# Edge weights of a message-passing layer: one product per tile on 64 rows of TensorE instead of a padded map

## The chip, the cores and the metric

One core of one Trainium2 chip. Its engines work side by side, each through its own list of instructions: PE (TensorE, matrix products; PEld is its loading of the stationary operand), DVE (VectorE), ACT (ScalarE), POOL (GpSimd) and SP (SyncE). Everything is float32. The metric is the device time of one execution in microseconds; the time given for a kernel is the median of several.

## The reference

There are 12,500 nodes with 160 features (64 scalars and 32 vectors of 3) and 400,000 edges, sorted by their target. Cut to what matters:

```python
h_s = s @ lin1_ws * a * inv(64)                  # per node
h_v = einsum('nci,cd->ndi', v, lin1_wv) * a * inv(32)
hid = silu(edge_scalars @ fc_w1 * inv(64))       # per edge, 64 numbers
w = hid @ fc_w2 * inv(64)                        # per edge, 224 edge weights
w1, w2, w3, w4, w5 = split(w, [64, 128, 160, 192])
es, ev = h_s[edge_src], h_v[edge_src]            # rows gathered by source
m_s1 = w1 * es * e0;  m_s2 = w4 * (ev . e1) * inv(3)
m_v1 = (w2 * es) x e1;  m_v2 = w3 * ev * e0;  m_v3 = w5 * cross(ev, e1) * inv(2)
agg = segment_sum(concat(m...), edge_dst) / 4    # 96 + 3*128 numbers per node
o = agg @ lin2 * a
y = layernorm(x + gate(self_connection + o))
```

`e0` and `e1` are an edge's four attributes. The change concerns the line `w = hid @ fc_w2`.

## The kernel before

**Start.** The node products `h_s`, `h_v` (L349, L359) are written as one table `h_tab` of 12,500 rows of 160 numbers to DRAM. POOL issues these writes, and after them the first gathers. DVE scales the map `fc_w2` into `w2` (L386), and subtracts the bases of blocks from the targets of all edges (`rel`, L420), which has to wait for `dt`, the targets.

**Tiles, chunks, quads.** A tile is 128 edges. Three tiles form a block, whose sums go into a window of 16 nodes. A chunk is 24 tiles, two halves of 12: half 0 holds the first 12 tiles, half 1 the next 12. The 64 inputs of half 0's edges lie on partitions 0 to 63 of `es`, those of half 1 on 64 to 127, so that one product with a block-diagonal `w1` and one `silu` (L463, L465) give `hid` for eight tiles, again with half 0 on the rows 0 to 63 and half 1 on 64 to 127. A step of the main loop takes a quad: two tiles of each half, four in all; `quads` lists them, and the place in that list is the tile's slot. There are 782 steps for 3,125 tiles, and the last step has one tile.

**One step n**, in the order in which the loop writes the instructions; on each engine they run in that order:

- POOL: four indirect gathers of 128 rows of `h_tab` into `hg` (L472), by the source of each edge. `hg` has four buffers, so the gathers may run four quads ahead of their use. In every 40th step (19 of them) the rows come by ordinary transfers instead, a row each, on the queues of SP and ACT (`hq`, L508), spread over the steps before.
- PE: the edge weights (L534) into `pw`, which has two buffers, so step n waits for DVE to be done with step n-2. `pw` is 4 x 256 float32 per partition, a slot for each tile: 224 weights, and 16 columns in which DVE writes the one-hot of targets (L597).
- DVE: the one-hot, the products `pr` of weights and gathered rows (L544 and three of L552), the select matrix `sel` (L606), and the addition of finished blocks into `acc` (L645).
- PE: the sums over targets of step n-2 (L613): each tile's `sel` (128x64) times its `pr` (128x416) into 64 of 128 partitions of `pa`, half 0's tiles into the first 64 and half 1's into the others, in turn.
- In every second step PE and ACT make `hid` for step n+2. When a block of each half is complete, ACT copies it (`sa`, L818), PE turns it (L622), ACT copies that (`tt`, L625, L627), and after 16 blocks PE applies `lin2` (L637). As nodes become complete, they are turned (L670), gated, normed and written out.

The stationary operand of the weights is `hid` of 128 rows, which has both halves' tiles one over the other. `w2` is therefore laid out twice with zeros: columns 0 to 223 have the map on rows 0 to 63, columns 224 to 447 have it on rows 64 to 127. One product of 128 rows and 448 columns then gives both tiles' weights, side by side in two neighbouring slots:

```python
nc.tensor.matmul(pw[:, t:t + m, :NWT], hid[:m * S, c * P:(c + 1) * P], w2[:m * S, :m], ...)
```

Of the kernel before, what the change touches and what calls it, by code (L numbers as in the profile page):

```python
# [10 lines left out]
F32 = mybir.dt.float32  # L11
# [10 lines left out]
P = 128  # L22
S = 64
# [12 lines left out]
CT = 2 * SIDE  # L36
# [11 lines left out]
NWT = 224  # L48
# [12 lines left out]
def gnn_kernel(  # L61
# [21 lines left out]
    nc = tc.nc  # L83
# [10 lines left out]
    consts = ctx.enter_context(tc.tile_pool(name="consts", bufs=1))  # L94
# [25 lines left out]
    def quads(halves):  # L120
        out = []
        for t in range(0, max(halves), 2):
            out.append([(half, u) for u in range(t, t + 2) for half in range(2) if u < halves[half]])
        return out


# [12 lines left out]
    for c, (_, halves) in enumerate(chunks):  # L139
        for i, slots in enumerate(quads(halves)):  # L140
            steps.append((c, i, [(tile_of(c, half, u), half, u) for half, u in slots]))
# [7 lines left out]
    def ahead(t):  # L149
        a0 = t // AHEAD * AHEAD  # L150
        if a0 not in aheads:
            n = min(AHEAD, TT - a0)
            idx = loads.tile([P, AHEAD], I32, name="idx")
            eat = loads.tile([P, AHEAD, 4], F32, name="eat")
            k = 0
            while k < n:
                g, u = divmod(a0 + k, GT)
                m = min(n - k, GT - u)
                nc.sync.dma_start(idx[:, k:k + m], src[g][:, u:u + m])
                nc.sync.dma_start(eat[:, k:k + m].rearrange("p t k -> p (t k)"),  # L160
                                  ea[g].rearrange("p t k -> p (t k)")[:, 4 * u:4 * (u + m)])
                k += m
            aheads[a0] = a0, idx, eat
        return aheads[a0]
# [5 lines left out]
    def by_slots(out, of, n, f):  # L170


        m = n // CT
        for u in range(SIDE if m else 0):
            o, i = out[:, 2 * u:2 * u + 1], of[:, u:u + 1]
            f(bass.AP(tensor=o.tensor, offset=o.offset,
                      ap=[o.ap[0], [CT * o.ap[1][0], m], [o.ap[1][0], 2], *o.ap[2:]]),
              bass.AP(tensor=i.tensor, offset=i.offset,
                      ap=[i.ap[0], [CT * i.ap[1][0], m], [SIDE * i.ap[1][0], 2], *i.ap[2:]]),
              u // BT, m)  # L180
        return m * CT
# [31 lines left out]
    w1 = consts.tile([2 * S, 2 * S], F32, name="w1")  # L213
    nc.vector.memset(w1, 0.0)

    w2 = consts.tile([2 * S, 2, NWT], F32, name="w2")
    nc.vector.memset(w2, 0.0)
    l2 = consts.tile([P, 11, V3], F32, name="l2")
    nc.vector.memset(l2, 0.0)
    share = ends_pool.tile([1, NB], I32, name="share")  # L220
# [10 lines left out]
    with tc.tile_pool(name="nodes", bufs=len(starts)) as nodes, tc.tile_pool(  # L231
        name="nodes_ps", bufs=6, space=PSUM
# [33 lines left out]
        for q in range(4):  # L266
            t0, s = divmod(q * QN, P)
            nc.gpsimd.dma_start(at_k[:P - s, q], attr[s:, t0:t0 + NQ])
            if s:
                m = min(NQ, NT - t0 - 1)  # L270
# [8 lines left out]
        at = consts.tile([P, NT], F32, name="at")  # L279
# [8 lines left out]
        halves = ends_pool.tile([P, 2], F32, name="halves")  # L288
# [32 lines left out]
        raw = ends_pool.tile([2 * S, NWT], F32, name="raw")  # L321
        for half in range(2):
            r = slice(half * S, (half + 1) * S)
# [14 lines left out]
        for c0, cn, xw, xz in loaded:  # L338
# [7 lines left out]
            n = min(cn, P)  # L346
# [32 lines left out]
    nc.vector.tensor_scalar_mul(half_at, at, 0.5)  # L379
    iota = consts.tile([P, W], F32, name="iota")  # L380
    nc.vector.tensor_copy(iota, iota_i)
    for half in range(2):
        r = slice(half * S, (half + 1) * S)
        at_c = 0
        for a, b in ((64, 128), (0, 64), (192, 224), (160, 192), (128, 160)):
            nc.vector.tensor_scalar_mul(w2[r, half, at_c:at_c + b - a], raw[r, a:b], 1.0 / math.sqrt(64))  # L386
            at_c += b - a

    scs = consts.tile([S, V3], F32, name="scs")
    nc.sync.dma_start(scs, sc_ws)  # L390
# [14 lines left out]
    for to, part, pieces, w, r0, c0, by in maps:  # L405
        for k, piece in enumerate(pieces):
# [3 lines left out]
            m = terms.setdefault((to, part, four), len(terms))  # L410
            at_r = at_p * V
            r = l2[at_r:at_r + V, m, c0:c0 + w.shape[1]]
# [11 lines left out]
    for t in range(by_slots(rel, dt, TT, relative), TT):  # L424
        nc.vector.tensor_tensor(rel[:, slot_of[t]:slot_of[t] + 1], dt[:, t:t + 1],  # L425
                                lo[:, t // BT:t // BT + 1], op=OP.subtract)
# [27 lines left out]
    def hidden(pool, psum, es, halves, t0, n):  # L454

        ph = psum.tile([2 * S, Q * P], F32, name="ph", tag="misc")
        hid = pool.tile([2 * S, Q * P], F32, name="hid")
        ends = [max(0, min(n, m - t0)) for m in halves]
        assert ends[0] >= ends[1]
        for k, c0, c1 in ((2 * S, 0, ends[1]), (S, ends[1], ends[0])):  # L460
            if c1 > c0:
                c = slice(c0 * P, c1 * P)
                nc.tensor.matmul(ph[:k, c], w1[:k, :k], es[:k, t0 * P + c0 * P:t0 * P + c1 * P],  # L463
                                 start=True, stop=True)
                nc.scalar.activation(hid[:k, c], ph[:k, c], AF.Silu, scale=1.0 / math.sqrt(64))  # L465
        return hid
# [59 lines left out]
    def weights(psum, hid, slots):  # L526

        pw = psum.tile([P, Q, 256], F32, name="pw")
        n = len(slots)
        for t in range(0, n, 2):  # L530
            half, c = slots[t]
            m = min(2, n - t)
            assert half == 0 and all(slots[t + k] == (k, c) for k in range(m))
            nc.tensor.matmul(pw[:, t:t + m, :NWT], hid[:m * S, c * P:(c + 1) * P], w2[:m * S, :m],  # L534
                             start=True, stop=True)
        return pw

# [33 lines left out]
    def by_slot(t):  # L571

        a0, _, eat = ahead(t)
        if a0 not in sorted_eat:
            n = min(AHEAD, TT - a0)
            eas = loads.tile([P, AHEAD, 4], F32, name="eas")
            m = n // CT
            for u in range(0, SIDE if m else 0, 2):
                o, i = eas[:, 2 * u:2 * u + 1], eat[:, u:u + 1]
                nc.scalar.copy(  # L580
                    bass.AP(tensor=o.tensor, offset=o.offset,
                            ap=[o.ap[0], [4 * CT, m], [8, 2], [4, 2], [1, 4]]),
                    bass.AP(tensor=i.tensor, offset=i.offset,
                            ap=[i.ap[0], [4 * CT, m], [4, 2], [4 * SIDE, 2], [1, 4]]))
            m *= CT
            for k in range(m, n):
                o = slot_of[a0 + k] - a0
                nc.scalar.copy(eas[:, o], eat[:, k])
            sorted_eat[a0] = eas
        return sorted_eat[a0]  # L590
# [10 lines left out]
    def select_quad(pool, tiles, oh):  # L601

        n = len(tiles)
        u = slot_of[tiles[0][0]] % AHEAD
        sel = pool.tile([P, Q, 4, W], F32, name="sel", bufs=3)
        nc.vector.tensor_mul(  # L606
            sel[:, :n], oh[:, :, None, :].to_broadcast([P, n, 4, W]),
            by_slot(tiles[0][0])[:, u:u + n, :, None].to_broadcast([P, n, 4, W]))
        return sel
# [108 lines left out]
    with tc.tile_pool(  # L718
        name="fin", bufs=1
    ) as fin, tc.tile_pool(  # L720
        name="mine", bufs=2
    ) as mine, tc.tile_pool(
        name="late", bufs=2
    ) as late, tc.tile_pool(name="edge", bufs=2) as edge, tc.tile_pool(
        name="deep", bufs=4
# [165 lines left out]
        with in_order:  # L891
# [6 lines left out]
            for n, (c, i, tiles) in enumerate(steps):  # L898
# [10 lines left out]
                fetch_rows(n)  # L909
                hg = hq_of.pop(n) if n in own else gather(deep, [index(t) for t, _, _ in tiles])  # L910
                pw = weights(pw_ps, hids[c, i // 2], [(half, u - i // 2 * 4) for _, half, u in tiles])

                rest = turning.pop(0)() if turning else None
# [46 lines left out]
            n = len(steps)  # L960
# [29 lines left out]
        with tc.For_i(0, n_redo, 1):  # L990
# [9 lines left out]
            with tc.For_i(0, n_again, 1) as g, tc.For_i(0, GT, 1) as k:  # L1000
                t = g * GT + k
# [19 lines left out]
                hid = hidden(edge, misc_ps, es, (1, 0), 0, 1)  # L1021
                hg = gather(deep, [idx])
                pr = products(edge, weights(pw_ps, hid, [(0, 0)]), hg, 1)
                r = edge.tile([P, 1], F32, name="r", bufs=1)
                had = edge.tile([P, 2], F32, name="had", bufs=1)
# [73 lines left out]
```

## Time and profile before

| | us |
|---|---|
| median of 3 runs | 3920.53 (3918.47 to 3926.07) |
| the profiled execution | 3915.52 |
| span of its instructions | 3913.8 |
| PE busy | 3634.4 (93%) |
| POOL busy | 2915.6 (74%) |
| DVE busy | 2441.2 (62%) |
| ACT busy | 895.3 (23%) |
| granted clock of TensorE, mean | 0.972 |

A row of a timeline has the start and the length of a piece of work in us, the engine, the line, the operation, what it writes and reads, its shape and how often it follows on itself; in square brackets stands how long the engine was idle before it and what ended that. A row of a group has, behind the bar, the busy time in us and the mean in ns of one, then the idle time ahead of it. A float32 product leaves two records on PE.

### The profile page before, as it was taken

The page shows a single profiled execution, that of the slowest core. Times are in us where ns is not written, and L with a number is a line of the kernel's source. Part 1 is how long each engine was busy: PE and PEld are TensorE (multiplying, and loading weights), DVE is VectorE, ACT ScalarE, POOL GpSimd, SP SyncE. Part 2 cuts the span into 40 slices and gives each one's busy share as a digit, 9 for nine tenths or more (in the row PEclk, how much of TensorE's full clock was granted, in tenths as well). Part 3 has the DMA queues.
Part 4 walks back from the last instruction along what each step waited for, and adds up shares of the span by engine and source line. Part 5 has one row for each costly group of instructions (what it writes and reads, how often), then busy time and mean ns, then how long its engine had stood idle before and what let it go on. Part 6 is the DMA issues. An engine that isn't in the chain of part 4 may idle for free. (4 is left out here: it accounts for less than half of the span.)

```text
span 3913.8 us, 66881 instructions
## 1 busy us (share of the span) xinstructions
PE 3634.4 (93%) x14293; PEld 1589.8 (41%) x14293; DVE 2441.2 (62%) x6532; ACT 895.3 (23%) x2481; POOL 2915.6 (74%) x3096
## 2 busy tenths in 40 slices
PE   6899999999989999899899999989999999989998
PEld 4344344344334444344344343434444344334443
DVE  6656566666655666656566666656666665656655
ACT  2222222222222222222222222222222222222222
POOL 6777777777777777777777777777777777777774
PEclk8999999999999999999999999999999999999999
DMA  7344444444344443443444444444343443444432
GB/s 241 97 104 104 101 105 101 101 105 105 101 105 103 105 108 99 104 109 98 103 106 103 101 109 101 102 103 107 101 111 98 101 112 98 102 103 100 104 99 65
DMA packets 258055, 413.16 MB, mean 106 GB/s; under 512 B 92568, under 2 KB 186273, under 8 KB 257509
## 3 DMA queue, kind: packets, MB, share of 16 engines
q0 software_dynamic: 149312, 260.41, 25.7%
q1 hardware_dynamic: 98004, 145.13, 15.1%
q10 hardware_dynamic: 10322, 3.26, 0.4%
q14 instruction: 302, 2.47, 0.2%
q8 instruction: 115, 1.88, 0.2%
HBM read 392.53 MB, written 16.00 MB: 104 GB/s over the span
## 5 line engine op out<-in xcount | busy, mean ns | idle before, releaser
L472 POOL DMA_INDIRECT hg<-h_tab,idx x3049 | 2885.1, 946 | 942.6 <-issue 834.8
L534 PE MATMUL pw<-w,hid 128*128 128x448 f32 x3126 | 1346.2, 554 | 29.3 <-ACT hid L465 10.8
L613 PE MATMUL pa<-pr,sel 128*64 128x416 f32 x6250 | 1287.4, 533 | 0.2 <-ACT sa L818 0.2
L552 DVE TENSOR_TENSOR pr<-pw,hg 128x384 f32<-128x384 f32 x2289 | 1125.7, 547 | 0.0
L597 DVE TENSOR_TENSOR pw<-rel,iota 128x64 f32<-128x64 int16 x782 | 181.4, 232 | 956.4 <-PE pw L534 953.4
L534 PEld LDWEIGHTS pw<-w,hid 128*128 128x128 f32 x3126 | 553.5, 193 | 487.4 <-issue 420.3
L544 DVE TENSOR_TENSOR pr<-pw,hg 128x512 f32<-128x512 f32 x763 | 527.1, 691 | 346.3 <-DMA hg<-h_tab,idx 250.9
L613 PEld LDWEIGHTS pa<-pr,sel 128*64 128x64 f32 x6250 | 384.4, 138 | 799.0 <-issue 772.9
L818 ACT COPY sa<-pa 128x416 f32<-128x416 f32 x521 | 262.8, 505 | 1081.3 <-DMA hq<-h_tab 612.7
L463 PE MATMUL misc<-es,w 128*128 128x512 f32 (+1 forms) x784 | 446.2, 651 | 20.3 <-DVE rel L425 17.7
L465 ACT ACTIVATE hid<-misc 128x512 f32<-128x512 f32 x392 | 233.5, 596 | 784.0 <-DMA hq<-h_tab 379.3
L622 PEld LDWEIGHTS misc<-ident,sa 128*128 128x128 f32 x2084 | 242.8, 143 | 383.9 <-issue 254.9
L622 PE MATMUL misc<-ident,sa 128*128 128x128 f32 x2084 | 334.1, 284 | 69.2 <-ACT hid L465 56.6
L637 PE MATMUL misc<-tt,l 128*96 128x256 f32 (+5 forms) x1496 | 360.7, 390 | 32.9 <-DVE y L683 26.9
L606 DVE TENSOR_TENSOR sel<-pw,eas 128x256 f32<-128x256 f32 x782 | 324.3, 415 | 9.5 <-ACT eas L580 9.3
L637 PEld LDWEIGHTS misc<-tt,l 128*96 128x96 f32 (+1 forms) x1496 | 233.8, 168 | 179.1 <-issue 98.3
L625 ACT COPY tt<-misc 128x192 f32<-128x192 f32 x521 | 164.6, 316 | 559.8 <-DMA hq<-h_tab 371.4
L463 PEld LDWEIGHTS misc<-es,w 128*128 128x128 f32 x784 | 118.4, 190 | 282.9 <-issue 229.8
L645 DVE TENSOR_TENSOR acc<-acc,os 96x32 f32 x1042 | 195.6, 188 | 25.3 <-ACT os L640 6.8
L627 ACT COPY tt<-misc 128x64 f32<-128x64 f32 x521 | 117.1, 225 | 0.0
L670 PE MATMUL misc<-ident,acc 96*128 96x96 f32 x196 | 35.5, 266 | 77.2 <-DVE pw L597 46.4
L640 ACT COPY os<-misc 96x512 f32<-96x512 f32 (+2 forms) x68 | 38.3, 563 | 208.6 <-PE misc L637 202.3
(89 smaller groups left out, 672.8 us busy)
## 6 DMA issues: line engine op xcount, KB each, us to landing
es<-in_es_t_dram SPq DMA_DIRECT2D x258, 384.0 KB
hq<-h_tab SPq DMA_DIRECT2D x4864, 0.6 KB
hq<-h_tab ACTq DMA_DIRECT2D x4864, 0.6 KB
hg<-h_tab,idx POOLq DMA_INDIRECT x3049
h_tab<-ht POOLq DMA_DIRECT2D x24, 320.0 KB
xt<-in_x_dram SPq DMA_DIRECT2D x23, 320.0 KB
out_dram<-y SPq DMA_DIRECT2D x23, 320.0 KB
xv<-in_xv_t_dram SPq DMA_DIRECT2D x25, 187.5 KB
```

The lines of the kernel that those rows point to most:

```text
L463: nc.tensor.matmul(ph[:k, c], w1[:k, :k], es[:k, t0 * P + c0 * P:t0 * P + c1 * P], start=True, stop=True)
L465: nc.scalar.activation(hid[:k, c], ph[:k, c], AF.Silu, scale=1.0 / math.sqrt(64))
L472: nc.gpsimd.indirect_dma_start(out=hg[:, t, :], out_offset=None, in_=h_tab, in_offset=bass.IndirectOffsetOnAxis(ap=i, axis=0))
L534: nc.tensor.matmul(pw[:, t:t + m, :NWT], hid[:m * S, c * P:(c + 1) * P], w2[:m * S, :m], start=True, stop=True)
L544: nc.vector.tensor_mul(two, pw[:, :n, :2 * S].rearrange("p t (k c) -> p t k c", k=2), hg[:, :n, None, :S].to_broadcast([P, n, 2, S]))
L552: nc.vector.tensor_mul(pr[:, :n, first:first + V3].rearrange("p t (i c) -> p t i c", i=3), pw[:, :n, None, 2 * S + k * V:2 * S + (k + 1) * ...
L606: nc.vector.tensor_mul(sel[:, :n], oh[:, :, None, :].to_broadcast([P, n, 4, W]), by_slot(tiles[0][0])[:, u:u + n, :, None].to_broadcast([P ...
L613: nc.tensor.matmul(pa[half * ROWS:(half + 1) * ROWS, :NPR], sel[:, t].rearrange("p k w -> p (k w)"), pr, start=start, stop=stop)
L622: nc.tensor.transpose(pt[:, four * P:four * P + k], sa[:k, c:c + P], ident[:k, :k])
L637: nc.tensor.matmul(po[:, k, :nb], l2[r, terms[to, part, four]], a[:, :nb], start=(n == 0), stop=(n == len(of) - 1))
L645: nc.vector.tensor_add(window, window, os[:, :, b])
L818: nc.scalar.copy(sa, pas.pop(j)[:, :NPR])
```

## The change

The map `w2` is kept without zeros: once on rows 0 to 63 and once on rows 64 to 127, 224 columns. Each tile has a product of its own, of the 64 rows of its half and 224 columns. `quads` now lists both tiles of half 0 and then both of half 1, so the slots 0 and 1 of `pw` belong to half 0 and the slots 2 and 3 to half 1; the products are issued in the order of tiles u, half 0 before half 1, which is slots 0, 2, 1, 3. The lists that go by slots (`rel`, and the attributes `eas`) are written in the new order, and the gathers of a quad follow it. The sums over targets keep their order.

```diff
     def quads(halves):
         out = []
         for t in range(0, max(halves), 2):
-            out.append([(half, u) for u in range(t, t + 2) for half in range(2) if u < halves[half]])
+            out.append([(half, u) for half in range(2) for u in range(t, t + 2) if u < halves[half]])
         return out
...
         for u in range(SIDE if m else 0):
-            o, i = out[:, 2 * u:2 * u + 1], of[:, u:u + 1]
+            at = u // 2 * 4 + u % 2
+            o, i = out[:, at:at + 1], of[:, u:u + 1]
             f(bass.AP(tensor=o.tensor, offset=o.offset,
-                      ap=[o.ap[0], [CT * o.ap[1][0], m], [o.ap[1][0], 2], *o.ap[2:]]),
+                      ap=[o.ap[0], [CT * o.ap[1][0], m], [2 * o.ap[1][0], 2], *o.ap[2:]]),
...
-    w2 = consts.tile([2 * S, 2, NWT], F32, name="w2")
-    nc.vector.memset(w2, 0.0)
+    w2 = consts.tile([2 * S, NWT], F32, name="w2")
...
-    for half in range(2):
-        r = slice(half * S, (half + 1) * S)
-        at_c = 0
-        for a, b in ((64, 128), (0, 64), (192, 224), (160, 192), (128, 160)):
-            nc.vector.tensor_scalar_mul(w2[r, half, at_c:at_c + b - a], raw[r, a:b], 1.0 / math.sqrt(64))
-            at_c += b - a
+    at_c = 0
+    for a, b in ((64, 128), (0, 64), (192, 224), (160, 192), (128, 160)):
+        nc.vector.tensor_scalar_mul(w2[:, at_c:at_c + b - a], raw[:, a:b], 1.0 / math.sqrt(64))
+        at_c += b - a
...
         pw = psum.tile([P, Q, 256], F32, name="pw")
-        n = len(slots)
-        for t in range(0, n, 2):
-            half, c = slots[t]
-            m = min(2, n - t)
-            assert half == 0 and all(slots[t + k] == (k, c) for k in range(m))
-            nc.tensor.matmul(pw[:, t:t + m, :NWT], hid[:m * S, c * P:(c + 1) * P], w2[:m * S, :m],
+        for t, (half, c) in sorted(enumerate(slots), key=lambda k: (k[1][1], k[1][0])):
+            r = slice(half * S, (half + 1) * S)
+            nc.tensor.matmul(pw[:, t, :NWT], hid[r, c * P:(c + 1) * P], w2[r],
                              start=True, stop=True)
         return pw
...
-                            ap=[o.ap[0], [4 * CT, m], [8, 2], [4, 2], [1, 4]]),
+                            ap=[o.ap[0], [4 * CT, m], [4, 2], [8, 2], [1, 4]]),
```

## The prediction

> **What bounds the kernel now.** I read the page first, for shares and groups, then everything about the gather line, then timelines of the start, the steady part and the end.
>
> ```profile
> span 3913.8 us, 66881 instructions
> PE 3634.4 (93%) x14293; PEld 1589.8 (41%) x14293; DVE 2441.2 (62%) x6532; ACT 895.3 (23%) x2481; POOL 2915.6 (74%) x3096
> ...
> L534 PE MATMUL pw<-w,hid 128*128 128x448 f32 x3126 | 1346.2, 554 | 29.3 <-ACT hid L465 10.8
> ...
> L606 DVE TENSOR_TENSOR sel<-pw,eas 128x256 f32<-128x256 f32 x782 | 324.3, 415 | 9.5 <-ACT eas L580 9.3
> ```
>
> And of the view of waits:
>
> ```profile
> DVE pw L597 <- PE pw L534: 953.4, 601, 9.7
> ```
>
> By the shares PE is the bound; L534, the line that is changed, is its largest group, and DVE's longest wait is for it (953.4 us in 601 times). The view of the gather line L472 says otherwise:
>
> ```profile
> L472 POOL DMA_INDIRECT hg<-h_tab,idx x3049: 940/946/1100, 51.2 to 3874.5; - x191
> ...
>   issue: 834.8, 2720
> ```
>
> A gather takes 0.946 us and POOL then sits 0.31 us (834.8 / 2720) in "issue", waiting for nothing that the trace shows. The stretches view over 480 gathers, cut at gather starts (columns: us, then busy us and count of PE, PEld, DVE, ACT, POOL, then clock, DMA share, GB/s):
>
> ```profile
> core 0: us, PE busy (x) PEld busy (x) DVE busy (x) ACT busy (x) POOL busy (x), PEclk, DMA share, GB/s
> 2410.90:3011.44 600.54, 564.25 (x2206) 243.13 (x2206) 376.39 (x1002) 134.97 (x386) 454.13 (x480) 0.98 0.41 102
> ```
>
> 600.54 / 480 = 1.251 us per gather. 3048 intervals of that are 3813.1 us; from first to last gather the rows give 3874.5 - 51.2 = 3823.3. So POOL stalls only 10.2 us in the whole run. The time is 51.2 (before the gathers) + 3813.1 + 10.2 + 39.3 (3913.8 - 3874.5). A faster PE can touch only the last two terms; nothing in the change shortens a gather, and their number stays 3049. Of the 10.2 us, two stalls as POOL's timeline shows them:
>
> ```profile
> 70.04 0.94 POOL L472 DMA_INDIRECT hg<-h_tab,idx  x1 [0.30 <-issue]
> 74.48 0.97 POOL L472 DMA_INDIRECT hg<-h_tab,idx  x1 [3.50 <-DVE l L307]
> ...
> 3524.89 0.95 POOL L472 DMA_INDIRECT hg<-h_tab,idx  x1 [0.30 <-issue]
> 3528.54 0.94 POOL L472 DMA_INDIRECT hg<-h_tab,idx  x1 [2.70 <-issue]
> ```
>
> The first is the start: four buffers `hg` are full, and gather 17 waits for the first products; 4.44 - 1.25 = 3.2 us. That leaves 7.0 us in the middle, of which the second pair is 2.4.
>
> **How far the consumers are behind.** DVE's products (L544) and POOL's gathers near the end:
>
> ```profile
> 3763.28 0.94 POOL L472 DMA_INDIRECT hg<-h_tab,idx  x1 [0.30 <-issue]
> ...
> 3868.29 0.95 POOL L472 DMA_INDIRECT hg<-h_tab,idx  x1 [0.30 <-issue]
> ...
> 3873.29 0.94 POOL L472 DMA_INDIRECT hg<-h_tab,idx  x1 [0.30 <-issue]
> 3874.53 0.94 POOL L472 DMA_INDIRECT hg<-h_tab,idx  x1 [0.30 <-issue]
> ```
>
> ```profile
> 3765.93 0.69 DVE L544 TENSOR_TENSOR pr<-pw,hg 128x512 f32<-128x512 f32 x1 [1.83 <-DMA hg<-h_tab,idx]
> ...
> 3884.09 0.68 DVE L544 TENSOR_TENSOR pr<-pw,hg 128x512 f32<-128x512 f32 x1
> 3884.69 1.48 DVE L552 TENSOR_TENSOR pr<-pw,hg 128x384 f32<-128x384 f32 x3
> ...
> 3886.55 0.28 DVE L544 TENSOR_TENSOR pr<-pw,hg 128x128 f32<-128x128 f32 x1
> 3886.75 0.58 DVE L552 TENSOR_TENSOR pr<-pw,hg 128x96 f32<-128x96 f32 x3
> ```
>
> At 3765.93 DVE waits for the gather issued at 3763.28: 2.65 us from issue to use is the least. The last whole quad (gather 3873.29) is used at 3884.09, 10.8 us behind, 8.15 more than needed; the last tile 12.0 behind. This backlog, made by PE, is what the change can take from the end.
>
> **The product itself.** PE's timeline, one steady step and the last steps:
>
> ```profile
> 1002.84 1.67 PE L534 MATMUL pw<-w,hid 128*128 128x448 f32 x4
> ...
> 1004.44 1.62 PE L613 MATMUL pa<-pr,sel 128*64 128x416 f32 x8
> ...
> 1005.98 0.66 PE L622 MATMUL misc<-ident,sa 128*128 128x128 f32 x4
> ```
>
> ```profile
> 3878.13 1.67 PE L534 MATMUL pw<-w,hid 128*128 128x448 f32 x4
> 3879.73 1.62 PE L613 MATMUL pa<-pr,sel 128*64 128x416 f32 x8
> 3881.28 0.66 PE L622 MATMUL misc<-ident,sa 128*128 128x128 f32 x4
> ...
> 3885.51 0.64 PE L534 MATMUL pw<-w,hid 64*128 64x224 f32 x2
> 3886.10 2.44 PE L637 MATMUL misc<-tt,l 128*96 128x96 f32 x22
> 3888.38 0.60 PE L622 MATMUL misc<-ident,sa 128*128 128x128 f32 x4
> 3888.91 2.31 PE L613 MATMUL pa<-pr,sel 128*64 128x416 f32 x10
> ```
>
> One f32 product leaves two records. A quad's four records of 448 columns take 1.60 us (1002.84 to 1004.44): about 0.375 each and 0.1 to drain before L613. The kernel has one 64-row product already, its last: two records of 224 columns, 0.59 us (3885.51 to 3886.10), weight load and drain with it. A record of 224 columns streams half as long as one of 448, 0.187. After the change a quad has eight such records, four on rows 0-63 and four on rows 64-127. If the halves overlap, it is 0.59 + 2 x 0.187 = 0.96 us, and up to 0.1 more where the step before was a full-array one (a drain like that ahead of L613): 0.55 to 0.64 less per quad, some 470 us of PE over 781 quads. If they don't, 0.59 + 6 x 0.187 = 1.71 with loads hidden, and 4 x 0.59 = 2.36 with none hidden.
>
> I take the overlap, by the nearest row: L613's eight records (two column halves of the array, each with its own load) take 1.54 us (1004.44 to 1005.98); at 416/448 x 0.375 = 0.35 each, one after another, they would need 2.8. That is columns, not rows: no row here has two row halves at once. The Trainium skill (TensorEngine Tiling (Array Packing), Key Properties and Gotcha 1) says that tiles operate in parallel, and that different row tiles cannot use one PSUM bank together; the new listing puts slots 0, 1 (half 0) and 2, 3 (half 1) into different 2 KB of `pw`. By that page the sum is the 0.96; no run here shows it.
>
> **What it is worth, end by end.** Beginning:
>
> ```profile
> 67.69 3.35 PE L534 MATMUL pw<-w,hid 128*128 128x448 f32 x4 [0.69 <-ACT hid L465]
> ```
>
> ```profile
> 58.30 6.23 DVE L420 TENSOR_TENSOR rel<-dt,lo 128x260 int16<-128x260 int32 x12 [11.79 <-DMA dt<-in_dst_dram]
> ...
> 71.08 0.23 DVE L597 TENSOR_TENSOR pw<-rel,iota 128x64 f32<-128x64 int16 x1 [6.22 <-PE pw L534]
> ```
>
> At the slow clock of the start the first product takes 67.69 to 71.08. Half the columns on the path are 1.5 us less, and POOL's stall of 3.2 shrinks by that: -1.5 (ends 0 and -3.2). Middle: consumers that run 2.65 us behind instead of 6 to 12 seldom fill four buffers. But the stall at 3524.89 comes from ACT, which the change doesn't touch:
>
> ```profile
> 3508.60 11.50 ACTq L508 DMA_DIRECT2D hq<-h_tab  x9
> 3520.20 0.60 ACT L465 ACTIVATE hid<-misc 128x512 f32<-128x512 f32 x1 [11.18 <-DMA hq<-h_tab]
> ```
>
> Nine row transfers hold ACT's queue for 11.5 us, and `hid` is late. Such a lump still fits into the buffers more often than now: -5 of 7.0 (ends 0 and -7). End: the last whole quad can be used at 3873.29 + 2.65 = 3875.94, 8.15 earlier. PE has then to be ready too. The quad before (last gather 3868.29) is used at 3870.94, and its products and select end 2.5 later (3884.09 to the end of L552 is 2.08, and 0.415 of L606): 3873.4. From there PE has L613 1.55, L622 0.66, the 64-row product 0.59, L637 2.28 and L622 0.53, 5.6 us, so L613 of the last quads could start at 3879.0 instead of 3888.91: 9.9 earlier. The last tile's products end at 3887.33 - 8.15 = 3879.2, in time for their place in that L613. I take -8.5, less by one half-clock stretch (below; 1.7 us), with the ends 0 and -9.9.
>
> Edits at nothing: ten scalings of `w2` become five and a memset goes, all ahead of DVE's wait of 11.79 for `dt`. The gathers, row transfers and eas copies change order, not number or size. The twelve `rel` subtractions (6.23 us, on the path to the first product) now write every second slot instead of pairs: taken as 0; ends -1 and +6. Eight weight loads instead of four are in the 0.59. The path after a failed margin doesn't run.
>
> Sum: 1.5 + 5 + 8.5 = 15.0 off a span of 3913.8: 3898.8; the profiled execution of 3915.52 becomes 3900.5. The median of the runs, 3920.53, lies 5.0 above that execution. What a run has beyond it can only be more stalls of POOL or a later end, the terms that shrink, so I let half of it go too: 3920.5 - 15 - 2.5 = **3903 us**, 0.45% less. 0.2% (7.8 us) is about what a measurement of this kernel can tell from no change.
>
> **Rivals.** *Halves one after another* (slower). PE idles 36.3 us in the 600.54 above, which is 120 gathered quads and 3 fetched otherwise: 0.295 us a step. A product over 1.60 + 0.295 = 1.90 us makes PE the bound. With every load exposed 2.36 + 0.09: 0.55 over, x 782 = 430 us: 4350. With loads hidden, 1.71 to 1.8, it stays under the point with 0.1 to 0.2 a step to spare; the backlog is cleared more slowly and the 7.0 us of stalls can double or treble: 3925 to 3940. For it: nothing shows row halves together; against: the column halves do it.
>
> *The clock gives it back.* PE will idle more. Successive stretches of 3.41 us:
>
> ```profile
> 1120.73:1124.14 3.41, 2.64 (x12) 1.18 (x13) 0.92 (x2) 1.45 (x5) 2.49 (x3) 1.00 0.38 110
> 1124.14:1127.55 3.41, 1.50 (x7) 0.59 (x7) 2.80 (x10) 0.43 (x2) 2.50 (x4) 1.00 0.22 62
> 1127.56:1130.97 3.41, 3.41 (x9) 0.99 (x6) 3.20 (x8) 0.22 (x1) 2.57 (x3) 0.50 0.28 74
> ```
>
> A stretch with PE busy 1.50 of 3.41 is followed by one at half clock. A light step after the change (0.96 + 1.55 of POOL's 5.0) leaves 2.5 us idle, so there will be more of these; each costs PE 1.7 us of work. Two at the end take 3.4 back (3906); if the whole gain of the end and the 2.5 of the median go, 3914. The skill (TensorE: Matmul & The Clock Gate, Part 1) names an idle window of about 3.4 us as the condition; the trace shows that a part-idle one does it, and that is what counts here.
>
> *The ends don't move.* Products in the end are held by something beside PE (accumulating, DMA landing), and start and middle bring under 7.8: 3913 to 3920.
>
> **How the numbers follow.** Forecast 0.64; clock 0.14 (0.10 of it beyond 7.8 us); ends 0.10; halves in turn 0.12. Faster 0.74, same 0.14, slower 0.12. Range: low with all ends at once, 3920.5 - 3.2 - 7 - 9.9 - 5 = 3895; high 3916, into the third rival; left out is the first and part of the third.
>
> **What would show it.** Right: L534 as 64x224, eight records in about 1 us with starts in pairs a few ns apart; gathers still 1.251 apart; first stall under 2; L544's last quad about 2.7 us after its gather; PE near 80%; more half-clock stretches. Wrong: starts of the records 0.19 or more apart, PE over 93%, DVE's wait for `pw` not below 953 us, or a last gap that stays at 10.

## The result, and the profile after

| | before | after |
|---|---|---|
| median of runs, first comparison, us | 3921.74 (3916.14 to 3926.07, 8 runs) | 3911.73 (3909.36 to 3912.68, 8 runs) |
| median of runs, a second chip, us | 3916.83 (3910.18 to 3920.85, 16 runs) | 3903.96 (3901.75 to 3904.91, 7 runs) |
| span of the profiled execution, us | 3913.8 | 3910.0 |
| PE, DVE, POOL busy, us | 3634.4, 2441.2, 2915.6 | 3322.2, 2413.3, 2925.1 |
| granted clock of TensorE, mean | 0.972 | 0.928 |

The ratio after / before is 0.9974 [0.9963, 0.9985] in the first comparison and 0.9967 [0.9956, 0.9979] on the second chip: faster, by 10.0 and 12.9 us, on both. The prediction was 3903. Two sets of the experiments ran on chips on which every kernel, the kernel before too, takes 5300 to 5700 us; their times are compared only with the kernel before on the same chip.

From the page of after, its head and two groups (busy us, mean ns, idle ahead and what ended it):

```profile
span 3910.0 us, 73124 instructions
PE 3322.2 (85%) x17417; PEld 1636.5 (42%) x17417; DVE 2413.3 (62%) x6526; ACT 894.0 (23%) x2481; POOL 2925.1 (75%) x3096
...
L470 POOL DMA_INDIRECT hg<-h_tab,idx x3049 | 2894.3, 949 | 935.3 <-issue 811.1
...
L529 PE MATMUL pw<-w,hid 64*128 64x224 f32 x6250 | 859.8, 391 | 194.8 <-DVE sel L601 98.7
```

From the view of waits of after (us in total, times, longest):

```profile
DVE pr L539 <- DMA hg<-h_tab,idx: 543.5, 261, 6.2
DVE pw L592 <- PE pw L529: 484.4, 264, 9.0
```

The lines have moved up by two to five: L529 is the weights product (L534 before), L470 the gather, L539 and L547 the products, L592 the one-hot, L418 the `rel` subtractions, L608 the sums, L506 the row transfers.

The weights product costs PE 859.8 us instead of 1346.2, 486 less. Other work takes 174 more of PE's busy time, some two thirds of it because it ran longer at half clock (below), and the busy time as a whole fell by 312 us. DVE waits for PE half as long (484.4 against 953.4), and its longest wait is now for the rows of the gathers. The run became only 4 us shorter in this profile. The gather line says why: 0.949 us per gather where the profile before had 0.946, with the same pause after it. The bound is the one of before, and in this profile it had itself become slower.

The stretch of 600.54 us in which the profile before had PE busy 564.25:

```profile
2410.90:3011.44 600.54, 519.30 (x2690) 253.47 (x2690) 368.06 (x992) 134.20 (x383) 454.36 (x480) 0.93 0.41 103
```

Again 480 gathers run in it, with PE idle 81 us in place of 36.

The product itself, in PE's timeline of after:

```profile
3863.16 1.03 PE L529 MATMUL pw<-w,hid 64*128 64x224 f32 x8
3864.11 1.62 PE L608 MATMUL pa<-pr,sel 128*64 128x416 f32 x8
```

Eight records follow on each other in 0.95 us, where four of 448 columns took 1.60. Single records show how: they start at 3863.155 and .162, .448 and .455, .637 and .644, .827 and .833. Two run at once, one per half. After the first pair, which has 0.29 to itself, a pair follows the one before by 0.19, the time of 224 columns. The Trainium skill (TensorEngine Tiling (Array Packing), Key Properties) says that different tiles can run LdWeights and Matmul in parallel; this trace agrees for row halves in float32, with 0.958 us per quad.

The start, on PE and DVE of after, and POOL's first stall:

```profile
70.13 1.86 PE L529 MATMUL pw<-w,hid 64*128 64x224 f32 x8 [0.69 <-ACT hid L463]
```

```profile
59.80 7.31 DVE L418 TENSOR_TENSOR rel<-dt,lo 128x260 int16<-128x260 int32 x12 [11.56 <-DMA dt<-in_dst_dram]
66.91 0.38 DVE L423 TENSOR_TENSOR rel<-dt,lo 128x1 int16<-128x1 int32 x5
```

```profile
72.04 0.94 POOL L470 DMA_INDIRECT hg<-h_tab,idx  x1 [0.30 <-issue]
75.48 0.95 POOL L470 DMA_INDIRECT hg<-h_tab,idx  x1 [2.49 <-DVE l L307]
```

The first product takes 1.86 in place of 3.35, and the stall is 2.19 beyond a normal interval, 3.2 before. The subtractions take 7.31 in place of 6.23.

The end, DVE and POOL and then PE, of after:

```profile
3877.60 0.95 POOL L470 DMA_INDIRECT hg<-h_tab,idx  x1 [0.30 <-issue]
3878.86 0.94 POOL L470 DMA_INDIRECT hg<-h_tab,idx  x1 [0.30 <-issue]
```

```profile
3880.38 0.68 DVE L539 TENSOR_TENSOR pr<-pw,hg 128x512 f32<-128x512 f32 x1
...
3882.72 0.28 DVE L539 TENSOR_TENSOR pr<-pw,hg 128x128 f32<-128x128 f32 x1
```

```profile
3884.76 2.31 PE L608 MATMUL pa<-pr,sel 128*64 128x416 f32 x10
```

The last whole quad is used 2.8 us after its gather (10.8 before), the last tile 3.9 (12.0 before), and the last sums start 5.9 us after the last gather (14.4 before). What lies behind the last gather fell from 39.2 to 31.1 us.

Where the 3.8 us of span went, from POOL's rows of both profiles: the first gather came 1.9 later (51.18 to 53.12; over all profiles here it lies between 51.2 and 53.3, without regard to the kernel); the stall of the start gave 1.0; the stalls of the middle (intervals over 1.3 us, less 1.251 each) fell from 7.7 to 2.5, which gave 5.2; the end gave 8.1. That is 14.3 less 1.9. Against it, the mean of the ordinary intervals is 1.25366 us in place of 1.25081: over 3048 of them, 8.7 us.

### The profile page after: what moved, and what is told of

Read it like the earlier page. It is cut to its first block, busy times and chain, and to the rows that moved or that the text cites. A ratio compares the mean times of both kernels' runs of the same rounds, so it can differ in the third digit from the quotient of the medians.

```text
span 3910.0 us, 73124 instructions
## 1 busy us (share of the span) xinstructions
PE 3322.2 (85%) x17417; PEld 1636.5 (42%) x17417; DVE 2413.3 (62%) x6526; ACT 894.0 (23%) x2481; POOL 2925.1 (75%) x3096
## 5 line engine op out<-in xcount | busy, mean ns | idle before, releaser
L470 POOL DMA_INDIRECT hg<-h_tab,idx x3049 | 2894.3, 949 | 935.3 <-issue 811.1
L608 PE MATMUL pa<-pr,sel 128*64 128x416 f32 x6250 | 1359.9, 559 | 1.8 <-ACT sa L813 1.8
L547 DVE TENSOR_TENSOR pr<-pw,hg 128x384 f32<-128x384 f32 x2289 | 1125.7, 547 | 0.0
L539 DVE TENSOR_TENSOR pr<-pw,hg 128x512 f32<-128x512 f32 x763 | 527.2, 691 | 816.6 <-DMA hg<-h_tab,idx 543.5
L529 PE MATMUL pw<-w,hid 64*128 64x224 f32 x6250 | 859.8, 391 | 194.8 <-DVE sel L601 98.7
L529 PEld LDWEIGHTS pw<-w,hid 64*128 64x128 f32 x6250 | 567.2, 195 | 493.8 <-issue 233.2
L608 PEld LDWEIGHTS pa<-pr,sel 128*64 128x64 f32 x6250 | 400.0, 143 | 579.5 <-issue 561.7
L461 PE MATMUL misc<-es,w 128*128 128x512 f32 (+1 forms) x784 | 465.9, 678 | 44.5 <-ACT tt L622 26.1
L592 DVE TENSOR_TENSOR pw<-rel,iota 128x64 f32<-128x64 int16 x782 | 180.2, 230 | 492.4 <-PE pw L529 484.4
L617 PE MATMUL misc<-ident,sa 128*128 128x128 f32 x2084 | 343.3, 289 | 131.2 <-ACT hid L463 102.2
L667 ACT ACTIVATE g<-misc,half_at 128x96 f32<-128x96 f32 x98 | 33.4, 341 | 224.0 <-PE misc L665 122.4
```

The lines of the kernel that those rows point to most:

```text
L470: nc.gpsimd.indirect_dma_start(out=hg[:, t, :], out_offset=None, in_=h_tab, in_offset=bass.IndirectOffsetOnAxis(ap=i, axis=0))
L529: nc.tensor.matmul(pw[:, t, :NWT], hid[r, c * P:(c + 1) * P], w2[r], start=True, stop=True)
L539: nc.vector.tensor_mul(two, pw[:, :n, :2 * S].rearrange("p t (k c) -> p t k c", k=2), hg[:, :n, None, :S].to_broadcast([P, n, 2, S]))
L547: nc.vector.tensor_mul(pr[:, :n, first:first + V3].rearrange("p t (i c) -> p t i c", i=3), pw[:, :n, None, 2 * S + k * V:2 * S + (k + 1) * ...
L608: nc.tensor.matmul(pa[half * ROWS:(half + 1) * ROWS, :NPR], sel[:, t].rearrange("p k w -> p (k w)"), pr, start=start, stop=stop)
L617: nc.tensor.transpose(pt[:, four * P:four * P + k], sa[:k, c:c + P], ident[:k, :k])
```

## The experiments

**The same two kernels on a second chip.** The question was whether the 3 ns per gather are the change's.

> The kernel before, unchanged. On the chip of the first four experiments every kernel took 5380 us or more, with register moves of 0.03 us on SP's queue that took up to 1.4 us there, so the question of the gather interval stayed open: both kernels had 1.2506 there. Theory A (0.003 us more per gather belongs to an execution or a chip, not to the kernel): on a chip where the kernel before takes about 3920, the two means of gather intervals agree to 0.001 us. Theory B: 1.2508 here and 1.2537 in the changed kernel.

> The changed kernel, unchanged. Theory A: the mean gather interval is that of the kernel before here to 0.001 us; the last gap is 31 against 39 us, the stalls of POOL 5 against 11 us, and the time 12 to 15 us less. Theory B: 0.003 us longer per gather, 8.7 us of the gain gone, 6 to 10 us less.

Before: 3914.49, ratio to the other runs of the kernel before 0.9996 [0.9987, 1.0006]. After: 3903.96, 0.9967 [0.9956, 0.9979]. The gather line and the last rows of POOL and DVE, after, on this chip:

```profile
L470 POOL DMA_INDIRECT hg<-h_tab,idx x3049 | 2885.5, 946 | 937.4 <-issue 818.7 <-DMA hg<-h_tab,idx 29.3 <-DVE pw L592 21.8
```

```profile
3869.11 0.95 POOL L470 DMA_INDIRECT hg<-h_tab,idx  x1 [0.30 <-issue]
3870.36 0.95 POOL L470 DMA_INDIRECT hg<-h_tab,idx  x1 [0.30 <-issue]
```

```profile
3873.32 0.68 DVE L539 TENSOR_TENSOR pr<-pw,hg 128x512 f32<-128x512 f32 x1
...
3875.66 0.28 DVE L539 TENSOR_TENSOR pr<-pw,hg 128x128 f32<-128x128 f32 x1
```

Here the changed kernel's gathers take 946 ns, as those of the kernel before. In the profiles of two other chips (below) the mean is 945.8 to 946.0 for all four kernels on the one, three of them with the new order, and 948.0 to 948.3 for all four on the other, each of them with the new order. The changed kernel itself has 949, 946 and 946 ns on three chips, so the 3 ns go with the chip and not with the change. No profile shows the kernel before on a chip with 948 or 949. Its median is 4.9 to 7.2 us higher in the first comparison than on the second chip, that of after 7.8, which fits a chip on which the gathers of both are slower. If so, the 8.7 us in the first pair of profiles are a difference of two chips, and the first pair's 14.3 less 1.9 us are what the change and chance gave.

The terms in this pair: stall of the start 4.10 to 2.59 (-1.5), middle 3.05 to 3.99 (+0.9, one stall of 2.1 at 1193.7 behind row transfers), end 37.7 to 32.8 (-4.9), gathers -0.5, first gather -0.1; together -6.0, the difference of the spans (3909.2 and 3903.1). The medians differ by 12.9, or by 10.5 from the ten runs that were made of the kernel before for this experiment (3914.49): the profiled execution of before lies 3.6 under that second median, that of after 0.9 over its own. The runs of before spread over 13.8 us here, those of after over 3.2.

**The two kernels on a chip with slow queues.**

> The kernel before, unchanged, profiled once more. In the first pair of profiles a gather plus its pause took 1.2508 us before and 1.2537 us after the change, 8.7 us over 3048 of them, though the change does not touch a gather. Theory A (the step belongs to the execution and not to the kernel): this profile may show 1.254 too, and the two kernels' means come closer than 0.001 us on one chip. Theory B (the change makes each gather longer): 1.2508 again here, and 1.2537 in the changed kernel beside it. By A the time here is some 3916 to 3926 us.

> The changed kernel, unchanged, beside the kernel before on one chip. Theory A: the mean of its gather intervals equals that of the kernel before here to 0.001 us, so that the difference of the two times is start, stalls and end alone: about 1 + 5 + 8 = 14 us less the slower subtractions (1.1 us) if the intervals agree. Theory B: its intervals are 0.003 us longer, and the difference stays at about 10 us.

Kernel before there: 5389.59 (5354.84 to 5414.81). Before again: 5380.58, 0.9987 [0.9962, 1.0012]. After: 5445.25, 1.0117 [1.0093, 1.0142], slower. The expectations were made for a chip on which the gathers bound the run. Here they don't. Waits of the kernel before on this chip, and one row of its queue for the row transfers (ns shortest, median, longest):

```profile
POOL hg L472 <- DVE pr L552: 1456.2, 322, 9.3
DVE pw L597 <- remote: 1116.6, 140, 14.1
PEld pa L613 <- issue: 927.9, 2245, 5.3
...
DVE pw L597 <- PE pw L534: 783.3, 219, 11.9
```

```profile
L508 SPq MOVE hq<-h_tab x4864: 1/29/1447, 95.7 to 5251.0; - x195
```

POOL waits 1456 us for buffers `hg`, in 322 times; in the profile before that row has 21.9 us in 58 times, most of it the ordinary pause of 0.3. A register move on SP's queue takes up to 1447 ns; in the profile before, the longest of the same 4864 takes 42:

```profile
L508 SPq MOVE hq<-h_tab x4864: 29/29/42, 89.3 to 3786.5; - x195
```

Of the 9,728 such moves on SP's and ACT's queues 1,144 take over 0.2 us, and none in the profile before. So queues stand still, for up to a microsecond and more at a time; PE seems to be among them (a load for the sums waits up to 5.3 us with nothing shown as its cause, 1.3 in the profile before), and POOL waits for its consumers. A gather still takes 946 ns.

**Only the new order, with the padded product.** Each tile has a product of its own of 128 rows and 224 columns, on the zero-padded map; the order, the `rel` pattern and the number of instructions on PE are those of after, but each product takes all 128 rows, so no two lie on different rows. The map is laid out twice with zeros again, as in the kernel before. The product's lines:

```diff
...
-            r = slice(half * S, (half + 1) * S)
-            nc.tensor.matmul(pw[:, t, :NWT], hid[r, c * P:(c + 1) * P], w2[r],
+            r = slice(0, 2 * S if (1, c) in slots else S)
+            nc.tensor.matmul(pw[:, t, :NWT], hid[r, c * P:(c + 1) * P], w2[r, half],
```

> The new order of tiles in a quad, but the products on 128 rows with the padded map, one tile of 224 columns each. My theory (the gain comes from PE's shorter products, which clear the backlog): a quad's products take about 1.6 us as before, the gap from the last gather to the end is again about 39 us, the stalls of POOL again about 10 us, and the time is that of the kernel before, plus 1 us for the subtractions that write every second slot: 3918 to 3928. Rival (the order of the tiles itself brings the gain, or lengthens the gathers): the gap at the end near 31 us, or gather intervals of 1.254 while the kernel before has 1.251 on this chip.

> The new order of tiles with products of 128 rows and the padded map, once more, where the kernel before takes about 3915. My theory (the whole gain is PE's shorter product): a quad's products take 1.6 us, the last gap is again 38 to 39 us, and the time is that of the kernel before and 1 us more (the subtractions into every second slot took 7.50 us instead of 6.56 in every profile of the new order). 3915 to 3922. Rival (the order of gathers brings part of the gain): 3905 to 3911 and a last gap under 35.

Measured on two slow chips: 5429.4, 1.0103 [1.0071, 1.0134], and 5368.22, 1.0084 [1.0053, 1.0115]. PE's timeline of the second:

```profile
2004.08 1.68 PE L532 MATMUL pw<-w,hid 128*128 128x224 f32 x8
2005.69 1.62 PE L611 MATMUL pa<-pr,sel 128*64 128x416 f32 x8
```

A quad takes 1.61 us, records starting 0.189 apart one by one. So shorter products alone save PE nothing, and the whole 0.65 us is the overlap. On these chips this kernel loses time too (40 and 38 us; after 56 on the first of the two, with intervals that overlap), though its products take as long as those of before. So what costs there is not the shorter product but something that both kernels have. The 6,248 more instructions on PE (3,124 each of loads and products) are the largest difference from the kernel before; that they are the cause is not shown.

**More products than needed.** Each 64-row product is issued two or three times into the same place, so the values are those of after.

```diff
-            nc.tensor.matmul(pw[:, t, :NWT], hid[r, c * P:(c + 1) * P], w2[r],
-                             start=True, stop=True)
+            for _ in range(2):
+                nc.tensor.matmul(pw[:, t, :NWT], hid[r, c * P:(c + 1) * P], w2[r],
+                                 start=True, stop=True)
```

> The changed kernel with each 64-row product issued twice into the same slot. If the row halves overlap, a quad's products take 0.96 + 0.75 = 1.71 us, 0.1 more than before the change. My theory (the gathers bound the run and the products only set how far the consumers lag): still under the 1.90 us from which PE would be the bound, so no more than 15 us over the kernel before: 3920 to 3940, the last gap back at about 39 us, and the mean clock back near 0.97. Rival (PE's length goes straight into the time): 782 x 0.75 = 590 us more than the changed kernel, 4500.

> The changed kernel with each 64-row product issued twice, 1.71 us a quad. My theory: PE has 0.295 us a step over 1.60 before it is the bound, so 1.71 only lengthens backlogs: 3920 to 3940, last gap 39 to 43. Rival (PE's time goes straight into the time): 0.75 x 782 = 590 us over the changed kernel.

Twice: 5597.12, 1.0404 [1.0374, 1.0434], and 5530.99, 1.0357 [1.0307, 1.0408]. The question was how much more product POOL's pace hides; for that the times are no answer, since POOL's pace isn't the bound on these chips. The durations are: 16 records in 1.82 us per quad, 0.1 over the 1.71 expected.

The same with three:

> The same with each product issued three times: 0.96 + 1.5 = 2.46 us a quad, 0.56 over the 1.90 from which PE should be the bound: my theory gives 0.56 x 782 = 440 us over the kernel before, 4350, with POOL waiting for DVE's products in most quads and PE over 95% busy. Rival (the gathers stay the bound, PE has more room than its busy time shows): under 4000.

5710.77, 1.07 [1.0653, 1.0747]. PE's timeline of it:

```profile
2014.19 3.02 PE L530 MATMUL pw<-w,hid 64*128 64x224 f32 x24
2017.14 1.27 PE L609 MATMUL pa<-pr,sel 128*64 128x416 f32 x6
```

24 records take 2.95 us. Their starts in this quad tell how far PE looks ahead: 2014.193, .486 and .676 are 0.29 and 0.19 apart, half 0 alone; the first record of half 1 starts at .681, a few ns after the third of half 0. Six records of half 0 stand ahead of it here, and it can start when three of them wait and one runs. With two (as in after) or four (next experiment) ahead it starts at once. At the other end the last two records run alone, 0.19 apart.

**Products in the order of slots.** Both tiles of half 0, then both of half 1, instead of halves in turn.

```diff
-        for t, (half, c) in sorted(enumerate(slots), key=lambda k: (k[1][1], k[1][0])):
+        for t, (half, c) in enumerate(slots):
```

> The changed kernel with the four products of a quad issued in the order of slots: both tiles of rows 0-63, then both of rows 64-127, instead of in turn. Theory A (PE looks only a few records ahead, so a half starts when it is issued next to one of the other half): the second half starts after three of the first half's four records, a quad's products take 1.4 to 1.7 us, and the time is within 8 us of the kernel before. Theory B (each half has a queue of its own that takes all four records): 0.96 us as in the changed kernel, and its time, 3904.

5366.93, 1.0068 [1.0045, 1.0091], beside 1.0117 [1.0093, 1.0142] for after on the other slow chip and 1.0084 for the padded products on this one. Its timeline:

```profile
2005.35 1.03 PE L529 MATMUL pw<-w,hid 64*128 64x224 f32 x8
2006.31 1.62 PE L608 MATMUL pa<-pr,sel 128*64 128x416 f32 x8
```

The quad takes 0.964 us, and its records start in pairs 13 ns apart in place of 7. Four records of half 0 ahead of the first of half 1 delay it by 13 ns, two by 7. So the halves overlap whichever order is written, as long as no more than four records of one half stand in a row; taking the halves in turn is not what makes the product short.

**Fewer gathers.** If gathers bound the run, 20 fewer should be worth 25 us. Every 32nd step takes its rows by ordinary transfers instead of every 40th, in the changed kernel and in the one before:

```diff
-OWN = 40
+OWN = 32
...
-SLOTS = (4, 3, 4, 3)
+SLOTS = (5, 4, 4, 4)
```

> The changed kernel, but every 32nd quad instead of every 40th has its rows brought by single transfers (24 quads instead of 19, 17 transfers issued per step instead of 14), so that POOL issues 20 gathers less. My theory (the gathers bound the run and PE has room): 5 x 5.0 = 25 us less than the changed kernel, about 3887, with the last gap still near 31. Rival (ACT's and SP's queues, which issue the single transfers, hold the rest up): stalls of POOL of 10 us and more come back, and the gain is under 12 us.

> The same with the kernel before. PE idles 36.3 us per 600.54 us there; taking 25 us of gathers out of 3813 leaves PE some 0.26 us of a step instead of 0.295. My theory: it gains too, but less, since PE clears the backlogs more slowly: 10 to 22 us less than the kernel before, 3900 to 3912, with more stalls of POOL and the last gap at 39 or more. Rival (PE's room doesn't matter at all): the full 25 us, as in the changed kernel.

After with it: 4208.67, 1.0751 [1.0733, 1.0769]; before with it: 4244.54, 1.0836 [1.0817, 1.0855]; both on the second, fast chip. There are 3029 gathers of 0.946 us, as meant, but POOL stalls 325 us in 162 intervals (after) and 366 in 193 (before). Waits of after with it (532.2 and 683.6 for the first two without it, on the same chip), and ACT in one step:

```profile
DVE pw L592 <- PE pw L529: 1237.6, 545, 13.3
ACT sa L813 <- DMA hq<-h_tab: 1059.9, 360, 7.9
...
POOL hg L470 <- DVE pr L547: 341.3, 174, 6.7
```

```profile
2009.74 5.39 ACTq L506 DMA_DIRECT2D hq<-h_tab  x9
2015.17 0.32 ACT L620 COPY tt<-misc 128x192 f32<-128x192 f32 x1 [6.06 <-DMA hq<-h_tab]
```

ACT issues nine transfers for 5.4 us, and has been idle for 6.06 us when the copy behind them starts. `hid` is late in the same way (its wait behind row transfers is 608.7 us in place of 464.6), PE's product with it, and POOL waits for DVE. The 25 us were not to be had: with 17 row transfers a step in place of 14, ACT's own work is late behind them. That the queues of ACT and SP are the price is what the rival had said, at a price far too low. One thing follows for the change: with POOL made to wait for the consumers, the changed kernel is 36 us faster than the one before, where it was 13. PE's room counts for more where something else makes the steps late. That is so on this chip; on the slow ones, where POOL waits too, the changed kernel lost.

## Why the prediction was right, and where not

The kernel is faster, and the traces show the mechanism that was named: PE's products are shorter, and stalls and end shrink, while the gathers go on as before. The size was forecast too large: 17.5 us off the kernel before, where 10.0 came in the first comparison and 12.9 (or 10.5) on the second chip. In the first comparison 3903 is 8.7 under the median of 3911.7, within the range. That it was met to 1 us on the second chip (3904.0) is luck in part: the kernel before takes 3916.8 or 3914.5 there, not the 3920.5 from which the sum started.

*The product, 1.60 to 0.96 us a quad.* Right: 0.958, by overlap, with pairs of starts 7 ns apart. No extra drain shows: the sums start 0.958 us after the first record at the median. The 470 us of PE time came out at 486. PE near 80% was wrong (85%), because its other work took 174 us more (see the clock, below).

*Gathers bound the run.* Right that nothing in the change touches them. Wrong that 1.251 would stand in every run: on some chips a gather takes 3 ns more, 8.7 us in all. The sum had no term for this, and the range was wide enough for other reasons. It need not be what was missed, though it has the same size: if the kernel before is slowed alike on that chip, as the medians suggest, the difference of the two kernels doesn't hold it, and the sum of the other terms was too large for the median run.

*Start, -1.5.* Measured -1.0 and -1.5, but not by that working; that the second agrees is luck. The term that was wrong is the one which put the twelve `rel` subtractions at 0. They and the five small ones behind them took 6.56 us (58.30 to 64.86, before) and take 7.49 (59.80 to 67.29), each large one in records of 0.80 us that start 0.60 apart, in place of 0.60 and 0.51; PE's first product for `hid` waits for the last of them, so the 0.9 us is on the path, as the bound of +6 had allowed. The product gave 1.49, so the change itself is worth 0.55 there. The sign that was given, a first stall under 2, wasn't met: 2.2 and 2.6. The rest came from the landing of `dt`, which let the subtractions start 0.4 and 1.0 us earlier after the first gather than in the profile of before on either side.

*Middle, -5 of 7.0.* Measured -5.2 and +0.9 in the two pairs of profiles. One execution holds few of these stalls, so a single pair settles little. The spread of the runs speaks for the mechanism: before 9.9, 10.7 and 13.8 us, after 3.3 and 3.2. Around the stall that was left on the second chip, 2.1 us behind the gather at 1193.7, these are ACT, PE and POOL of after:

```profile
1185.84 3.29 ACTq L506 DMA_DIRECT2D hq<-h_tab  x5
1189.22 0.51 ACT L813 COPY sa<-pa 128x416 f32<-128x416 f32 x1 [3.91 <-DMA hq<-h_tab]
1189.31 0.57 ACTq L506 DMA_DIRECT2D hq<-h_tab  x2
1189.92 0.60 ACT L463 ACTIVATE hid<-misc 128x512 f32<-128x512 f32 x1 [0.19 <-DMA hq<-h_tab]
```

```profile
1190.57 1.98 PE L793 MATMUL misc<-xv,scv 96*96 96x500 f32 x2 [3.64 <-ACT hid L463]
1192.48 1.86 PE L529 MATMUL pw<-w,hid 64*128 64x224 f32 x8
...
1194.27 2.50 PE L608 MATMUL pa<-pr,sel 128*64 128x416 f32 x8
```

```profile
1193.67 0.95 POOL L470 DMA_INDIRECT hg<-h_tab,idx  x1 [0.30 <-issue]
1197.01 0.95 POOL L470 DMA_INDIRECT hg<-h_tab,idx  x1 [2.40 <-DVE pr L547]
```

`hid` is late behind row transfers, which the prediction named as untouched, and PE idles 3.64 us for it. Then PE is at half clock (0.50 from 1189.3 to 1196.1): the two records of L793 take 1.91 us until the product starts, and the product 1.79 until the sums, in place of 1.01 and 0.96 at full clock. So some 1.7 of the 2.1 us is what the clock added, an estimate from these rows.

*End, -8.5.* Measured -8.1 and -4.9. In the first pair the last whole quad follows its gather by 2.8 us (2.7 forecast), and the last sums start 8.5 us closer to the last gather. In the second the quad is used at 4.2, and the last sums start 6.1 us closer. The quad before it is late there: DVE waits for its weights, and uses it 5.5 us after its gather (2.7 in the first pair). DVE and PE of after on the second chip:

```profile
3869.37 0.23 DVE L592 TENSOR_TENSOR pw<-rel,iota 128x64 f32<-128x64 int16 x1 [1.19 <-PE pw L529]
```

```profile
3867.71 0.66 PE L617 MATMUL misc<-ident,sa 128*128 128x128 f32 x4
3868.29 1.03 PE L529 MATMUL pw<-w,hid 64*128 64x224 f32 x8
...
3877.88 2.31 PE L608 MATMUL pa<-pr,sel 128*64 128x416 f32 x10
```

PE works without a pause between these rows, so the end is still PE's, which comes to the quad later than in the first pair; why was not settled. From this product (3868.29) to the start of the last sums (3877.88) PE takes 9.6 us in both profiles of after and 10.8 in both of before: that 1.2 us is the two shorter products themselves, and the rest is that PE comes to them earlier. The forecast held the least lag to be the lag; it is the best case. By its own working (9.9 less 1.7) the term would have been 8.2, not 8.5.

*The half of 5.0 let go for the median.* Right in kind: runs of after lie within 3.3 us of each other and the profiled one on their median.

*Rivals.* "Halves one after another" is refuted by 0.958 us; the padded products show what it would have looked like, 1.61 and single starts. "The clock gives it back" is half right: stretches of half clock went from 38 (218 us) to 96 (563 us). From the stretches view of after:

```profile
116.53:119.94 3.41, 0.96 (x7) 0.72 (x9) 2.42 (x5) 1.39 (x4) 2.50 (x4) 1.00 0.28 70
119.94:123.36 3.42, 3.42 (x16) 1.45 (x12) 1.48 (x4) 0.43 (x2) 2.50 (x4) 0.50 0.24 63
```

A window with PE busy 0.96 of 3.41 us, and then one at half clock. Of the single stretches after the start in this profile, each follows a window in which PE was busy less than half (on the second chip one follows a window with 0.53). PE's other work is busy at half clock for 350 us, 117 before; half of the difference, 116 us, is an estimate of what the slower clock took of the 174. The rest is that the records of the product and of other work overlap less, 113 us in place of 167. PE has 588 us idle, and at the end, where the rival put the loss, none fell between 3858 and 3891 us. What they cost the run is what they add to a stall that has another cause, as the 1.7 us above. "The ends don't move" fell with the 8.1 us.

*What stays open.* How much of the gain on a fast chip is owed to the overlap and how much to the mere order, and where the limit of hidden product time lies (1.90 us a quad by the prediction): the kernels for it ran on slow chips only. Seen directly as the shorter product's are 1.49 us at the start and 1.2 at the end. Why queues stand still there isn't settled. Time grows along with PE's instructions: the kernels of the new order, with 6,248 more, take 37 to 56 us longer than the kernel before, and doubling the products, another 12,500, gives +152 over after on the one chip and +163 over the padded products on the other. That the queues run short of instructions would fit, and was only argued: the packets of the DMA queues for instructions take no longer there (medians 0.97 and 0.35 us in the kernel before, 1.06 and 0.44 in the profile before), and doubled products also hold PE longer.

## What to carry to other kernels

Find the engine that is busy without a wait from first to last, and sum its intervals; a 93% engine beside it is worth only the stalls and the end that it causes, here 10 to 13 of 486 us of PE time saved. Two products of 64 rows on the two halves of TensorE run at once, so the zero-padded block map costs 1.60 us a quad where 0.96 is enough; shorter products alone don't bring that (1.61), and both orders of issue that were tried do (0.958 and 0.964). An edit in the order of a list can move the write pattern of an operation at the start of the path: price it from the pattern, not from its size.

## What the runs showed of the hardware that was not expected

- A 64-row product starts beside the other half's though up to four records of the first half stand ahead of it (13 ns late); with six ahead it starts 0.49 us late.
- 260 int16 results per partition in pairs that lie side by side follow each other on DVE every 0.51 us, written to every second place every 0.60 (records of 0.60 and 0.80).
- The indirect gather of 128 rows takes 946 ns on some chips and 948 to 949 on others, uniformly: 8.7 us or 0.2% of the run, nearly as much as this change is worth.
- On some chips a register move on a queue takes up to 1.4 us where it takes 29 ns, the same kernel takes 37% longer (5389.59 against 3921.74), and on one of them a change that saves PE time and adds PE instructions turns from 0.3% faster to 1.2% slower.
